# A conditioned linear layer and a mixture of experts: gathered rows kept in two column halves, left-half products first, and the matrix engine's expert stage ordered by hand

## The chip, the cores and the metric

The kernel runs on one core of a Trainium2 chip. The time is that of the device, in microseconds (us), for one execution; lower is better. Several executions are timed, and one more is recorded by the hardware profiler, from which all rows below come. The engines are PE (TensorE, the matrix engine; its weight loads are shown as PEld), DVE (VectorE), ACT (ScalarE), POOL (GpSimd) and SP (SyncE, which here only issues DMAs). Each engine takes its instructions in the order in which they stand in its program, and an instruction waits for the semaphores that it names.

## The reference

There are four sequences of 1024 tokens with 512 columns. Each sequence is multiplied by a weight matrix picked by its category, and a bias is added. The result goes through a mixture of 8 experts with 512 slots each: a router picks one expert per token, tokens get a rank among those with the same expert, those of rank 512 and more are dropped, and each expert does two layers (512 to 2048, ReLU, 2048 to 512). The output is weighted by the probability of the choice and added to the input.

```python
xl = einsum('bsd,bdh->bsh', x, W[cat]) + b[cat][:, None, :]
xf = xl.reshape(4096, 512)
probs = softmax(xf @ Wr); eidx = argmax(probs); p_tok = probs[eidx]
rank = (number of earlier tokens with the same expert)
keep = rank < 512                       # 512 slots for each of 8 experts
xe = xf[dispatch]                       # [8, 512, 512], rows by expert and slot
h  = maximum(einsum('ecd,edf->ecf', xe, W1), 0)
ye = einsum('ecf,efd->ecd', h, W2) * p_tok[dispatch] * valid
out = x + scatter(ye)
```

All is float32.

## The kernel before, in words

**Seven products.** Every matrix product is done by a scheme with seven block products in place of eight (Strassen's, in Winograd's form): both operands are cut into two by two blocks, sums and differences of the blocks are made first (`sums`, `differences`, `sum_w`, `sum_w1`, `sum_w2`, on DVE), and the products k = 1 to 7 are added up in three PSUM banks called x, y and z (`BANK`). Products 1, 6, 7 and 4 go, in this order, into bank x. Between them the bank is copied out (by DVE in `linear`, by ACT in `first_layer`), so product 6 can be added only when the copy after product 1 is done, 7 after the copy of 6, and 4 after that of 7. Product 2 has bank z; 5 and 3 share bank y.

**Linear stage** (lines 178 to 537). PE and SP follow an order written by hand: `ORDER` lists, for one sequence b, pairs (g, k) of a half g of its tokens and a product k, and `beside` says what PE does after each of the fourteen (transposes of x and of the weights, the router, `choose` and `rank`). A block of the result that is finished is written by SP into `xc_dram` in HBM (`done`), a row of which has 512 columns. `choose` (DVE) picks the expert of each of 1024 tokens, and builds up counts `past`, one step of 128 x 8 numbers after the other; `rank` needs two PE products with these counts, and then POOL scatters (token, probability) pairs into `slots` in HBM, eight indirect DMAs for each sequence. After the last sequence `keep_warm` lets PE do seven products on zeros.

**Between the stages** (lines 539 to 546). ACT's queue loads `slots` into `table`, POOL makes row numbers of it, and `gather` (POOL, indirect DMAs) fetches the 512 rows of expert 0 from `xc_dram`, 128 at a time into a tile of 128 x 512. `transpose_rows` transposes them on PE, four 128 x 128 blocks for each tile, and DVE copies them out (L610) and makes the differences.

**Expert stage** (lines 704 to 747). Here only SP's order is by hand. The order of PE, DVE, ACT and POOL is made by the framework's scheduler, from dependencies and estimates, and need not be that of the text. For each expert, `first_layer(e, g, k)` runs over four groups g of hidden columns with seven products of eight passes each (four matmuls; a float32 matmul is recorded as two passes). `second_layer(e, k)` has seven products in two halves of sixteen passes each, one for `at` = 0 and one for `at` = 1, that lie in the same PSUM bank:

```python
for at in range(HC):                  # L671, HC = 2
    for m in range(NG * HB):
        nc.tensor.matmul(ps[:, at, :], ...)
    if k in (1, 2):
        add(ps, 0, at, 0)             # DVE, L667: rows += ps * probability
```

After each half, `add` (DVE, L667) reads the bank and adds it to the rows; for k = 7 two such additions follow (bank x and bank y), for k = 5 none. The framework makes a write into a bank wait for the reads of it that stand before it in the text, though they are of the other half. Among the second-layer products stand the last two first-layer products of the expert (k = 4 and 3 of group 3) and `transpose_rows` of the next expert, and the scheduler laid such work between the two halves of a product. `fetch` gathers, early in each expert, its input rows and the next expert's rows (eight indirect DMAs on POOL).

The functions that the change touches, with their line numbers:

Of the kernel before, what the change touches and what calls it, by code (L numbers as in the profile page):

```python
# [22 lines left out]
def kernel(  # L23
# [97 lines left out]
    xc_dram = dram.tile([T, D], F32, name="xc_dram")  # L121

    table = const.tile([P, E, SC, ROW], F32, name="table")
# [54 lines left out]
    with (  # L178
# [7 lines left out]
        tc.tile_pool(name="xco", bufs=1) as xco,  # L186
# [184 lines left out]
        def rank(b):  # L371
# [12 lines left out]
            nc.vector.scalar_tensor_tensor(at, best, -float(CAP), r, ALU.mult, ALU.add)  # L384
            dest = rt.tile([P, GT], I32, tag="dest", bufs=B, name=f"dest_{b}")
            nc.vector.scalar_tensor_tensor(dest, at, float(E * CAP), over, ALU.add, ALU.add)
# [13 lines left out]
        def linear(b, g, k):  # L400
# [3 lines left out]
            ps = bank(ps_x, key, k, [P, 2, HD], "xc", bufs=2 if BANK[k] == "x" else 1)  # L404
# [20 lines left out]
            def block(i, j):  # L425
                return xco.tile([P, 2, HD], F32, tag=f"c{i}{j}", name=f"xc{i}{j}_{c}")

            def done(t, i, j):
                at = c * CT + i * HT
                nc.sync.dma_start(  # L430
                    out=xc_dram[at : at + HT, j * HD : (j + 1) * HD].rearrange(
                        "(j p) d -> p j d", p=P
                    ),
                    in_=t,
                )

            if k in (1, 6, 7):
                banks[key, k] = parts.tile([P, 2, HD], F32, tag=f"s{k}", name=f"s{k}_{b}_{g}")
                plus_bias(banks[key, k], 0 if k == 1 else 1)
            if k in (2, 3):  # L440
                t = block(0, int(k == 3))
                latest[0] = nc.vector.tensor_tensor(
                    t, ps, banks.pop((key, 1 if k == 2 else 6)), ALU.add
                )
                done(t, 0, int(k == 3))
            if k == 7:
                t = block(1, 1)
                nc.vector.tensor_tensor(t, banks[key, "y"], banks.pop((key, 7)), ALU.add)
                done(t, 1, 1)
            if k == 4:  # L450
                t = block(1, 0)
                plus_bias(t, 0)
                done(t, 1, 0)
# [5 lines left out]
        )  # L459

# [38 lines left out]
            (2, 7): [(X, 3, 6)],  # L499
            (2, 8): [(X, 3, 7), (RS, 3, 0)],  # L500
            (2, 9): [(behind, sum_w, 3)],
            (2, 10): [(R, 3, 1)],
            (2, 12): [(RS, 3, 1), (choose, 3)],
            (2, 11): [(behind, sum_w1, 0, 0)],
            (3, 2): [(rank, 3)],
            (3, 4): [(behind, sum_w1, 0, 1)],
            (3, 7): [(behind, sum_w1, 0, 2)],
# [12 lines left out]
        with tc.manual_schedule(engines={mybir.EngineType.PE, mybir.EngineType.SP}):  # L520
# [11 lines left out]
            for b in range(B):  # L532
                for i, (g, k) in enumerate(ORDER):
# [3 lines left out]
            keep_warm(ps_t, 7)  # L537

        nc.scalar.dma_start(
            out=table.rearrange("p e c r -> p e (c r)"),  # L540
            in_=slots.rearrange("(e p c) r -> p e (c r)", e=E, c=SC),
        )

        token = table.rearrange("p e c r -> p (e c) r")[:, :, 1]
        nc.gpsimd.tensor_scalar(src_row, token, FAR, float(T - 1), ALU.add, ALU.min)
        nc.gpsimd.tensor_scalar(dst_row, token, FAR, None, ALU.add)
# [32 lines left out]
    def gather(e, pool, source, into, at):  # L579
        for c in range(SC):  # L580
            n = e * SC + c
            into[n] = pool.tile([P, D], F32, tag="rows", name=f"rows_{n}")
            nc.gpsimd.indirect_dma_start(  # L583
                out=into[n],
                out_offset=None,
                in_=source,
                in_offset=bass.IndirectOffsetOnAxis(ap=at[:, c : c + 1], axis=0),
            )

    def fetch(e):  # L590
# [4 lines left out]
        gather(e, xr, xf, residual, at[:, 0:SC])  # L595
# [3 lines left out]
    def transpose_rows(e, c):  # L599

        if c == 0:
            xes[e] = xep.tile([P, 7, HK, HC * P], F32, tag="xe", name=f"xe_{e}")
        t = xes[e]
        r = rows.pop(e * SC + c)
        ps = ps_e.tile([P, KC, P], F32, tag="t", name=f"ps_e_{e}_{c}")
        for kc in range(KC):
            nc.tensor.transpose(ps[:, kc, :], r[:, kc * P : (kc + 1) * P], ident)  # L607

        half, at = divmod(c, HC)
        nc.vector.tensor_copy(  # L610
            t[:, 2 * half : 2 * half + 2, :, at * P : (at + 1) * P].rearrange(
                "p b k n -> p (b k) n"
            ),
            ps,
        )
        if c == SC - 1:
            differences(nc.vector, *(t[:, k, :, :] for k in (0, 2, 1, 3, 4, 5, 6)))
# [6 lines left out]
    def first_layer(e, g, k):  # L624
# [16 lines left out]
        if k in (1, 6, 7):  # L641
            banks[key, k] = snap.tile([P, HB, HC * P], F32, tag=f"s{k}", name=f"s{k}_{e}_{g}")
# [16 lines left out]
    def second_layer(e, k):  # L659
# [4 lines left out]
        def add(ps, half, at, part):  # L664
# [3 lines left out]
                row, ps[:, at, :], table[:, e, half * HC + at, 0:1], row, ALU.mult, ALU.add  # L668
# [35 lines left out]
    with tc.manual_schedule(engines={mybir.EngineType.SP}):  # L704
        gather(0, xg, xc_dram, rows, src_row)
        for c in range(SC):
            transpose_rows(0, c)
        for e in range(E):
            for g in range(NG):
                first_layer(e, g, 1)  # L710
                first_layer(e, g, 2)
                if g > 0:
                    first_layer(e, g - 1, 4)
                    first_layer(e, g - 1, 3)
                    ahead = e * NG + g - 1 + W1G
                    if ahead < E * NG:
# [62 lines left out]
```

## Time and profile before

| | |
|---|---|
| median of 3 runs | 971.0 us (967.38 to 971.63) |
| the profiled execution | 969.31 us, its span 967.5 us |
| mean granted PE clock in it | 0.995 of full speed |
| PE busy | 950.1 us, 98% of the span |
| DVE, ACT, POOL busy | 472.7, 171.0, 139.1 us |
| HBM | read 105.96 MB, written 25.23 MB |
| linear stage | from the start to about 153 us |
| one expert | 99.0 us (expert 1 begins at 272.01, expert 2 at 371.04) |
| last PE instruction | ends at 962.3 us |

A page of the profile gives the busy time of each engine, the groups of instructions, and what ended the idle time before an instruction. In the rows of the order of time, the first number is the start in us, the second how long it took, then engine, line of the program, operation, the tiles (written<-read) with buffer numbers left out, and in brackets idle time of the engine just before it with what ended it. Ends of matmuls are modelled and overlap the next start by some 0.15 us, so the pace of PE is read from starts.

### The profile page before, as it was taken

What the parts mean: (1) busy time and instruction counts of PE and PEld (TensorE: products, weight loads), DVE (VectorE), ACT (ScalarE), POOL (GpSimd) and SP (SyncE); (2) the same over time, 40 slices, a digit from 0 to 9 for tenths busy, and PEclk for the clock granted to TensorE, in tenths of its full rate; (3) what the DMA queues carried; (4) which work ended last, traced back from release to release, by engine and by line L of the source; (5) the groups of instructions that cost most, each with busy time, mean ns of one, the idle gap of its engine ahead of it and who ended that gap; (6) DMA issues with size and microseconds to landing.
All of it is one profiled execution on the core that took longest, in us unless ns stands there. A gap on an engine that the chain in (4) does not pass through costs nothing.

```text
span 967.5 us, 11249 instructions
## 1 busy us (share of the span) xinstructions
PE 950.1 (98%) x4570; PEld 812.2 (84%) x4570; DVE 472.7 (49%) x822; ACT 171.0 (18%) x289; POOL 139.1 (14%) x141
## 2 busy tenths in 40 slices
PE   9999988999999999999999999999999999999997
PEld 5788776888888888888888888888888888888886
DVE  4656574374337522762276317731673157325621
ACT  3233200320023002310231013101320132003200
POOL 0043332200022001200130013001300130012001
PEclk9999998999999999999999999999999999999999
DMA  9389223399134313532253225313532352332001
GB/s 323 115 166 227 90 81 93 132 400 337 60 131 159 131 55 114 173 107 74 84 175 127 82 93 174 130 48 128 174 101 73 127 174 71 104 126 87 1 0 44
DMA packets 95509, 123.18 MB, mean 127 GB/s; under 512 B 8820, under 2 KB 82548, under 8 KB 95266
## 3 DMA queue, kind: packets, MB, share of 16 engines
q1 hardware_dynamic: 85042, 97.54, 31.6%
q0 software_dynamic: 8704, 24.85, 7.8%
q8 instruction: 36, 0.59, 0.2%
q10 hardware_dynamic: 1712, 0.08, 0.1%
q14 instruction: 15, 0.12, 0.1%
HBM read 105.96 MB, written 25.23 MB: 136 GB/s over the span
## 4 chain that ended last, share of the span: by engine, by line
PE 58%; issue 17%; DVE 4%; DMA 2%; POOL 1%; SPq 1%; POOLq 0%; ACT 0%; DVEq 0%
PE hx L630 17%; PE yx L673 16%; PE yy L673 9%; PE hy L630 8%; PE hz L630 4%; PE yz L673 3%; DMA w_b<-in_L_ffn_W_dram 2%; PE ps_e L607 1%; POOL out_dram L694 1%; POOL rows L583 1%; SPq L566 1%; DMA rows<-xc_dram,src_row 0%; DVE h L150 0%; DVE h L151 0%; DVE h L149 0%
## 5 line engine op out<-in xcount | busy, mean ns | idle before, releaser
L630 PE MATMUL hx<-xe,w 128*128 128x256 f32 x1024 | 242.8, 382 | 1.4 <-ACT s L643 1.4
L630 PEld LDWEIGHTS hx<-xe,w 128*128 128x128 f32 x1024 | 195.3, 192 | 27.6 <-ACT s L643 1.8
L643 ACT COPY s<-hx 128x512 f32<-128x512 f32 x96 | 55.9, 582 | 437.7 <-PE hx L630 437.7
L630 PE MATMUL hy<-xe,w 128*128 128x256 f32 x512 | 122.1, 380 | 0.0
L673 PE MATMUL yx<-w_t,h 128*128 128x256 f32 x512 | 119.9, 380 | 1.2 <-DVE rows L667 1.2
L673 PE MATMUL yx<-w_b,h 128*128 128x256 f32 x512 | 116.6, 381 | 1.1 <-DVE rows L667 1.1
L694 POOL DMA_INDIRECT out_dram<-rows,dst_row x32 | 31.9, 998 | 572.1 <-DVE rows L667 572.1
L673 PEld LDWEIGHTS yx<-w_b,h 128*128 128x128 f32 x512 | 95.8, 190 | 16.5 <-DVE rows L667 3.7
L673 PEld LDWEIGHTS yx<-w_t,h 128*128 128x128 f32 x512 | 95.4, 190 | 15.9 <-DVE rows L667 2.0
L630 PEld LDWEIGHTS hy<-xe,w 128*128 128x128 f32 x512 | 97.4, 190 | 13.3 <-DVE h L646 0.4
L667 DVE SCALAR_TENSOR_TENSOR rows<-yx,table,rows 128x256 f32<-128x256 f32 x64 | 31.0, 484 | 140.2 <-PE yx L673 140.2
L647 ACT ACTIVATE h<-h 128x512 f32<-128x512 f32 x96 | 60.5, 630 | 203.0 <-DVE h L646 203.0
L646 DVE TENSOR_TENSOR h<-hy,s 128x512 f32<-128x512 f32 x64 | 44.2, 691 | 98.8 <-PE hy L630 54.8
L630 PE MATMUL hz<-xe,w 128*128 128x256 f32 x256 | 61.7, 380 | 0.0
L673 PE MATMUL yz<-w_b,h 128*128 128x256 f32 x256 | 58.7, 383 | 0.4
L673 PE MATMUL yy<-w_b,h 128*128 128x256 f32 x256 | 58.4, 381 | 0.0
L673 PE MATMUL yy<-w_t,h 128*128 128x256 f32 x256 | 57.9, 380 | 0.0
L583 POOL DMA_INDIRECT rows<-in_x_dram,at x32 | 40.2, 1257 | 122.7 <-DVE at L594 93.0
L673 PEld LDWEIGHTS yz<-w_b,h 128*128 128x128 f32 x256 | 48.1, 190 | 9.5 <-DVE rows L667 3.4
L630 PEld LDWEIGHTS hz<-xe,w 128*128 128x128 f32 x256 | 48.9, 191 | 6.6
L673 PEld LDWEIGHTS yy<-w_b,h 128*128 128x128 f32 x256 | 47.6, 190 | 8.1 <-DVE rows L667 1.4
L673 PEld LDWEIGHTS yy<-w_t,h 128*128 128x128 f32 x256 | 48.2, 190 | 6.2
(118 smaller groups left out, 894.7 us busy)
## 6 DMA issues: line engine op xcount, KB each, us to landing
w<-in_L_ffn_W_dram SPq DMA_DIRECT2D x64, 512.0 KB, 4.3
w_b<-in_L_ffn_W_dram SPq DMA_DIRECT2D x32, 1024.0 KB, 5.5
x<-in_x_dram SPq DMA_DIRECT2D x8, 1024.0 KB, 9.7
xc_dram<-xc SPq DMA_DIRECT2D x32, 256.0 KB, 4.1
out_dram<-in_x_dram SPq DMA_DIRECT2D x2, 2816.0 KB, 22.4
cw<-in_L_cond_W_dram SPq DMA_DIRECT2D x4, 1024.0 KB, 11.2
out_dram<-in_x_dram SPq DMA_DIRECT2D x1, 2560.0 KB, 16.0
cb<-in_L_cond_b_dram SPq DMA_DIRECT2D x4, 256.0 KB, 9.9
```

Source lines behind the costliest of these rows:

```text
L566: nc.sync.dma_start(out=t[k], in_=w2[e, i * F // 2 : (i + 1) * F // 2, j * D // 2 : (j + 1) * D // 2].rearrange("(m p) d -> p m d", p=P),)
L583: nc.gpsimd.indirect_dma_start(out=into[n], out_offset=None, in_=source, in_offset=bass.IndirectOffsetOnAxis(ap=at[:, c : c + 1], axis=0),)
L607: nc.tensor.transpose(ps[:, kc, :], r[:, kc * P : (kc + 1) * P], ident)
L630: nc.tensor.matmul(ps[:, j, :], lhsT=w1s[e, g][:, LEFT[k], kc, j * P : (j + 1) * P], rhs=xes[e][:, RIGHT1[k], kc, :], start=(k in OPENS an ...
L643: nc.scalar.copy(banks[key, k], ps)
L646: latest[0] = nc.vector.tensor_tensor(into, ps, part, ALU.add)
L647: nc.scalar.activation(into, into, AF.Relu)
L667: nc.vector.scalar_tensor_tensor(row, ps[:, at, :], table[:, e, half * HC + at, 0:1], row, ALU.mult, ALU.add)
L673: nc.tensor.matmul(ps[:, at, :], lhsT=hs[e, m // HB][:, LEFT[k], m % HB, at * P : (at + 1) * P], rhs=w2s[e][RIGHT2[k]][:, m, :], start=(k ...
L694: nc.gpsimd.indirect_dma_start(out=of, out_offset=bass.IndirectOffsetOnAxis(ap=dst_row[:, n : n + 1], axis=0), in_=residual.pop(n), in_off ...
```

## The change

- `xc_dram` is two tensors of 256 columns instead of one of 512. `gather` fetches rows in as many parts as it is given sources: all left halves, then all right halves, so the next expert's rows take eight indirect DMAs instead of four. The input rows are still fetched whole.
- `slots` and `table` are laid out with the expert innermost, and the index arithmetic in `rank` follows. Each partition loads one run of `slots` instead of eight.
- In `linear`, the finished blocks are added up in place in the tiles of the bank copies, which get two buffers; the pool `xco` goes. The last sequence has its own order (`ORDERS`): for each half of the tokens products 1, 2, 6, 7, 4, then 5, 5, 3, 3; with it, `choose` and `rank` of the last sequence move ahead in `beside`. The last product 5 has a bank in another pool. Two idle products follow the stage, not seven.
- `transpose_rows` can do the left or the right half of the columns alone. For expert 0 a loop does so three times, each followed or interrupted by products of groups 0 and 1: left halves with k = 1, left halves with k = 5, right halves with k = 2; products 4 and 3 and 6 and 7 of these groups follow from the main loop, whose middle part is now the function `between`.
- The bank copy after product 1 of the first layer has two buffers.
- In the expert stage PE's order, too, is that of the text.

```diff
-    xc_dram = dram.tile([T, D], F32, name="xc_dram")
-    table = const.tile([P, E, SC, ROW], F32, name="table")
+    xc_dram = [dram.tile([T, HD], F32, name=f"xc{j}_dram") for j in range(2)]
+    table = const.tile([P, SC, E, ROW], F32, name="table")
...
-            nc.vector.scalar_tensor_tensor(at, best, -float(CAP), r, ALU.mult, ALU.add)
+            nc.vector.scalar_tensor_tensor(at, r, float(E), best, ALU.mult, ALU.subtract)
...
-            ps = bank(ps_x, key, k, [P, 2, HD], "xc", bufs=2 if BANK[k] == "x" else 1)
+            if (b, g, k) == (B - 1, 1, 5):
+                banks[key, "y"] = ps_l.tile([P, 2, HD], F32, tag="m", name="xcy_last")
+                ps = banks[key, "y"]
+            else:
+                ps = bank(ps_x, key, k, [P, 2, HD], "xc", bufs=2 if BANK[k] == "x" else 1)
...
             if k in (2, 3):
-                t = block(0, int(k == 3))
-                latest[0] = nc.vector.tensor_tensor(
-                    t, ps, banks.pop((key, 1 if k == 2 else 6)), ALU.add
-                )
+                t = banks.pop((key, 1 if k == 2 else 6))
+                latest[0] = nc.vector.tensor_tensor(t, ps, t, ALU.add)
                 done(t, 0, int(k == 3))
-            if k == 7:
-                t = block(1, 1)
-                nc.vector.tensor_tensor(t, banks[key, "y"], banks.pop((key, 7)), ALU.add)
+            if k == (7 if b < B - 1 else 5):
+                t = banks.pop((key, 7))
+                nc.vector.tensor_tensor(t, banks[key, "y"], t, ALU.add)
...
+        ORDERS = [ORDER] * (B - 1) + [
+            [(g, k) for g in range(2) for k in (1, 2, 6, 7, 4)]
+            + [(g, k) for k in (5, 3) for g in range(2)]
+        ]
...
-            (2, 7): [(X, 3, 6)],
-            (2, 8): [(X, 3, 7), (RS, 3, 0)],
+            (2, 7): [(X, 3, 6), (X, 3, 7)],
+            (2, 8): [(R, 3, 1), (RS, 3, 0)],
             (2, 9): [(behind, sum_w, 3)],
-            (2, 10): [(R, 3, 1)],
-            (2, 12): [(RS, 3, 1), (choose, 3)],
+            (2, 10): [(RS, 3, 1), (choose, 3)],
             (2, 11): [(behind, sum_w1, 0, 0)],
-            (3, 2): [(rank, 3)],
-            (3, 4): [(behind, sum_w1, 0, 1)],
-            (3, 7): [(behind, sum_w1, 0, 2)],
+            (3, 0): [(rank, 3)],
+            (3, 5): [(behind, sum_w1, 0, 1)],
+            (3, 9): [(behind, sum_w1, 0, 2)],
...
-            keep_warm(ps_t, 7)
+            keep_warm(ps_t, 2)
...
-            out=table.rearrange("p e c r -> p e (c r)"),
-            in_=slots.rearrange("(e p c) r -> p e (c r)", e=E, c=SC),
+            out=table.rearrange("p c e r -> p (c e r)"),
+            in_=slots.rearrange("(p s) r -> p (s r)", p=P),
...
+    def gather(e, pool, sources, into, at):
+        n = D // len(sources)
+        for j, source in enumerate(sources):
+            for c in range(SC):
...
+                nc.gpsimd.indirect_dma_start(
+                    out=into[e * SC + c][:, j * n : (j + 1) * n],
...
+    def transpose_rows(e, c, parts=range(2)):
...
+        for kc in range(n * HK):
+            nc.tensor.transpose(ps[:, kc, :], r[:, (lo + kc) * P : (lo + kc + 1) * P], ident)
...
         if c == SC - 1:
-            differences(nc.vector, *(t[:, k, :, :] for k in (0, 2, 1, 3, 4, 5, 6)))
+            b11, b21, b12, b22, t1, t2, t4 = (t[:, k, :, :] for k in range(7))
+            if 0 in parts:
+                nc.vector.tensor_tensor(t1, b12, b11, ALU.subtract)
+            if 1 in parts:
+                nc.vector.tensor_tensor(t2, b22, t1, ALU.subtract)
+                nc.vector.tensor_tensor(b12, b22, b12, ALU.subtract)
+                nc.vector.tensor_tensor(t4, b21, t2, ALU.subtract)
...
-    with tc.manual_schedule(engines={mybir.EngineType.SP}):
+    with tc.manual_schedule(engines={mybir.EngineType.PE, mybir.EngineType.SP}):
         gather(0, xg, xc_dram, rows, src_row)
-        for c in range(SC):
-            transpose_rows(0, c)
+        for k, part in ((1, [0]), (5, [0]), (2, [1])):
+            for c in range(SC):
+                transpose_rows(0, c, part)
+                if (k, c) in ((1, HC - 1), (5, SC - 1), (2, HC - 1)):
+                    for g in range(2):
+                        first_layer(0, g, k)
         for e in range(E):
             for g in range(NG):
+                if e == 0 and g < 2:
+                    between(e, g)
+                    first_layer(e, g, 6)
+                    first_layer(e, g, 7)
+                    continue
                 first_layer(e, g, 1)
                 first_layer(e, g, 2)
...
+                between(e, g)
                 first_layer(e, g, 6)
```

## The prediction

> **What bounds the kernel now.** I read the engine table first, then the waits of the matrix engine (PE), then the order of time at the two places that the change rewrites. Page, head and engine table:
>
> ```profile
> span 967.5 us, 11249 instructions
> ...
> PE 950.1 (98%) x4570; PEld 812.2 (84%) x4570; DVE 472.7 (49%) x822; ACT 171.0 (18%) x289; POOL 139.1 (14%) x141
> ```
>
> PE is busy for 950.1 of 967.5 us, so time can be gained only in the remaining 17, or where PE is busy at a low clock or with idle products; whatever lets PE wait is added whole. PE in the view of waits (who waited for whom: us, times, longest):
>
> ```profile
> PE ps_e L607 <- DMA rows<-xc_dram,src_row: 2.5, 3, 1.4
> PE yx L673 <- DVE rows L667: 2.2, 4, 0.6
> ```
>
> The first row is the gather ahead of expert 0, the second the second layer waiting for VectorE (DVE) to read a bank. The order of time around the gather (start us, us, engine, line):
>
> ```profile
> 153.27 6.17 PE L69 MATMUL ps_idle<-idle 128*128 128x512 f32 x14
> 157.34 1.06 POOL L583 DMA_INDIRECT rows<-xc_dram,src_row  x1 [1.49 <-DMA xc_dram<-xc]
> 160.80 0.66 PE L607 MATMUL ps_e<-ident,rows 128*128 128x128 f32 x4 [1.36 <-DMA rows<-xc_dram,src_row]
> ...
> 168.90 1.94 PE L630 MATMUL hz<-xe,w 128*128 128x256 f32 x8
> ```
>
> and the clock there (stretch, us, busy us of PE, PEld, DVE, ACT, POOL, granted clock, DMA):
>
> ```profile
> 161.00:162.00 1.00, 0.46 (x4) 0.22 (x3) 0.50 (x1) 0.00 (x0) 0.79 (x1) 1.00 0.66 213
> 162.00:163.00 1.00, 0.70 (x4) 0.70 (x4) 0.19 (x1) 0.00 (x0) 0.16 (x1) 0.58 0.66 201
> ...
> 168.00:169.00 1.00, 1.00 (x4) 0.78 (x3) 0.97 (x3) 0.00 (x0) 0.00 (x0) 0.50 0.00 0
> 169.00:170.00 1.00, 1.00 (x6) 0.90 (x5) 0.96 (x2) 0.58 (x1) 0.00 (x0) 1.00 0.00 0
> ```
>
> A product of eight passes takes 1.726 us at full clock (303.09 to 311.72 holds five), four transposes 0.434. From the last linear product (153.27) to `hz` at 168.90 PE needs 1.74 + 1.73, so some 12 us are lost: gather, copies, half clock for 6.8 us. That is what can be won here.
>
> The other place is the second layer. Expert 2, first two products (k=1 and k=2, two halves each):
>
> ```profile
> 412.48 3.62 PE L673 MATMUL yx<-w_b,h 128*128 128x256 f32 x16
> 415.93 1.89 PE L630 MATMUL hx<-xe,w 128*128 128x256 f32 x8
> 417.65 1.03 PE L630 MATMUL hy<-xe,w 128*128 128x256 f32 x4
> 418.05 0.48 DVE L667 SCALAR_TENSOR_TENSOR rows<-yx,table,rows 128x256 f32<-128x256 f32 x1
> 418.59 3.72 PE L673 MATMUL yx<-w_b,h 128*128 128x256 f32 x16
> ...
> 423.01 3.62 PE L673 MATMUL yz<-w_b,h 128*128 128x256 f32 x16
> ...
> 428.76 0.48 DVE L667 SCALAR_TENSOR_TENSOR rows<-yz,table,rows 128x256 f32<-128x256 f32 x1
> 429.29 3.72 PE L673 MATMUL yz<-w_b,h 128*128 128x256 f32 x16
> ```
>
> The second half of a product never starts before L667 has read the first half (same bank): 418.53 to 418.59, 429.24 to 429.29. In between PE does first-layer products, transposes and the next product, put there by the scheduler. The last expert, with less to put there, shows the bare wait:
>
> ```profile
> 938.85 3.62 PE L673 MATMUL yx<-w_b,h 128*128 128x256 f32 x16
> 942.51 0.48 DVE L667 SCALAR_TENSOR_TENSOR rows<-yx,table,rows 128x256 f32<-128x256 f32 x1 [9.01 <-PE yx L673]
> ...
> 943.04 3.72 PE L673 MATMUL yx<-w_b,h 128*128 128x256 f32 x16 [0.58 <-DVE rows L667]
> ```
>
> The slot of sixteen passes ends at 938.85 + 3.45 = 942.30, the next starts at 943.04: 0.74 us.
>
> **The change, part by part.** The largest part is one word: PE joins the engines with an order by hand in the expert stage. In the built program the sixteen passes of each product then stand together, with no filler between halves.
>
> *Second layer.* Work and DVE's order up to each L667 are as before, so I take each wait from where L667 stands behind its producer. Of experts 1 to 6: k=1, half one ends at 415.93, half two starts at 418.59: 2.66 (DVE still has w2 sums and an h total ahead). k=2: L667 follows L630 k=3 by nine DVE operations (h total, four w1 sums, four h sums); from the end of k=3 (423.01) to half two (429.29) are 6.28, less half one, 3.45: 2.83. k=6, k=7, k=3 and k=4: 0.74 each, 2.96. k=5 has no reader. Half one of k=3 needs the second L667 of k=7, behind one L667 and one copy of transposed rows: 0.2 start + 0.53 + 0.60 + 0.48 + 0.05 = 1.86, less the four transposes, 0.43: 1.43. Sum 9.88 an expert, 59.3 for six. Expert 0: k=1 1.52 (217.48 to 219.00), k=2 229.94 - 225.15 - 3.45 = 1.34, the rest 4.39: 7.2. Expert 7 (no transposes, no w1 sums): 0.74 + 1.33 + 2.96 + 1.26 = 6.3. All 72.8. Before, this stretch runs from 214.03 to 962.0, 748.0 us; its products and transposes are 386.7 + 338.5 + 3.5 + 12.2 = 740.8; 7.2 of waits were there. **Net +65.6.** Bounds: with all waits bare 5.7 an expert, 46.6 in all, +39.4; above, the sum itself plus the clock.
>
> *Clock.* Idle of 1.36 and 0.84 us in the stretch before 162.2 let it fall to 0.50 for 6.8 us; two waits of 1.5 at 128.7 and 132.4 did not. Twelve waits of 2.66 or 2.83 are new. Bounds: none falls, 0; each falls for 6.8, 12 x 3.4 = +41. After 162.2 PE stayed partly idle for two more us; behind these waits it is full at once, so I take half the duration (3.4 us low, 1.7 lost). Whether a wait of 2.7 suffices lies between the 1.5 that did not and the 2.2 in two pieces that did, and may hang on where it falls in time, so I take half of the twelve: 6 x 1.7 = **+10**, an estimate.
>
> [...]
>
> *Last linear batch.* `choose` comes after (2,10) instead of (2,12), `rank` after (3,0): PE asks for `past` at 126.8, DVE has it at about 129.7 (its order still holds ten 0.6 us operations between the seven `past`), wait 2.9, as before (1.53 + 1.45). But k=6, 7, 4 now follow each other in one bank, each behind a 0.69 copy (L418): 0.2 + 0.69 + 0.05, 0.95 to 1.05 four times, 3.95. The stage ends at about 156.6 instead of 153.27. Bounds: two of the copies free, +1.4; DVE's w1 sums ahead of all, +6.
>
> *Scatter, table, gather.* The scatters start at about 131.8 (135.63 before): eight, 1.28 apart, last ends 142.0; the table load was issued 4.9 after that, src_row came 4.4 later: 151.3. The load in one 256 B run per partition instead of eight of 32 B may save up to 2 (shortest landing of an `xc_dram` write 2.1 against 4.3). Left halves of the rows are written by 153.75 (copy ends 150.6, landing 3.1 as at 154.2 to 157.34). Left gathers are issued 153.75 to 157.6, landing 157.2 to 161.1 (3.46 each); right ones, behind the write of k=3, from 160.65, landing 164.1 to 168.0.
>
> *Expert 0, from 156.6 to the first product of group 2* (189.67 - 1.73 = 187.95 before, 34.7 after the linear stage). Two idle products 1.73 (five dropped), twelve products 20.7, twelve pairs of transposes 2.6: the loop transposes the left half twice, as part [0] stands for k=1 and again for k=5. Waits: left copy 0.7; the second pass of left copies, two banks deep, 163.45 to 167.15 less its transposes 2.8; right copies 0.65; t2 behind two h totals and two copies 1.95; three bank snapshots with nothing between (k=6, 7, 4 of group 0, 6, 7 of group 1; copy 0.58) at 0.83, 2.5. Sum 33.7, so group 2 starts at 190.3, 2.3 late. A fall of the clock in the 2.8 us stretch is as likely as not: **+3**. Bounds: every wait hidden, 25.0 instead of 34.7, -9.7 + 3.3 = -6.4; clock low for 6.8 and right gather 3 late, +9.
>
> *At nothing:* index arithmetic (same two operations), in-place sums and second buffers (a buffer comes back after some 24 us, its write lands in 4.1), four more gathers per expert on POOL (4 x 1.27; POOL is 14% busy, the queue behind them is the output scatter, some 40 us later, and the transposes wait for rows landed 25 us earlier; if that cover went, 5 us an expert). SP's order keeps its transfers; w1 and w2 loads follow PE.
>
> Sum against the execution's own 969.31 (span 967.5 + 1.8, 1.7 below the median of 971.0 and inside 967.38 to 971.63): 969.3 + 65.6 + 10 + 3 = **1048 us**.
>
> **Rivals.** (a) Other side: PE's new order costs nothing per expert, since DVE is free in time, and the hidden gather decides: 969.3 - 6.4 = 963. It needs under 0.8 us an expert; one bare wait is 0.74, and there are six, so the three bare waits of the last expert speak against it. For it: DVE is 49% busy. (b) All waits bare, DVE having caught up: 969.3 + 39.4 + 3 = 1012. Against: DVE runs without a gap from 398 to 418. For: a slower PE leaves it time. (c) The clock falls at each long wait: 969.3 + 65.6 + 3 + 41 = 1079. For it: 2.2 us of idle sufficed at 162.2.
>
> **How the numbers follow.** Forecast 0.70 (1025 to 1066), (a) 0.03, (b) 0.12, (c) 0.12, anything else 0.03. The range 1018 to 1068 leaves out (a), (c) and half of (b), 2 in 10. About 0.5% is what a measurement can tell from no change: faster 0.03, same 0.01, slower 0.96.
>
> **What would show it.** Waits of yx, yy and yz for L667's counterpart: some 50, 60 to 75 us, against 2.2. In an expert, 2.7 and 2.8 us idle in k=1 and k=2, 0.74 in the others; from expert to expert 108 us (99.0 before: 272.01 to 371.04). Stretches of clock 0.50, about six. Linear stage ending near 156.6, left gather issued near 154, group 2 near 190. I am wrong if waits between halves are absent (then a), or 0.74 at k=1 and k=2 (b), or if an expert takes 108 but the clock never falls (969.3 + 65.6 + 3 = 1038).

## The result, and the profile after

The changed kernel takes 1055.65 us in the median of five executions (1055.23 to 1059.47), the kernel before, run beside it, 971.0 (967.38 to 971.87): 1.0886 times as long, 95% interval 1.086 to 1.0911. The forecast was 1048, with a range of 1018 to 1068. The profiled execution took 1055.48 us, 86.2 more than that of before (969.31).

The page of the changed kernel, span and engine table:

```profile
span 1053.7 us, 11265 instructions
...
PE 964.3 (92%) x4568; PEld 812.4 (77%) x4568; DVE 475.4 (45%) x831; ACT 171.2 (16%) x289; POOL 174.6 (17%) x173
```

PE is busy for 14 us more with the same products (eight more transposes, five fewer idle products), and the span has grown by 86: what is new is that PE stands still. The view of waits of PE says for whom (line 694 is the second layer's product, 688 the DVE instruction that reads its bank; us, times, longest):

```profile
PE yx L694 <- DVE rows L688: 30.8, 32, 2.5
PE yz L694 <- DVE rows L688: 18.3, 8, 2.7
PE yy L694 <- DVE rows L688: 13.9, 16, 1.2
PE hx L649 <- ACT s L664: 3.7, 4, 1.7
PE xcx_lin L413 <- DVE s L423: 3.5, 4, 1.0
PE rk L375 <- DVE past L356: 2.5, 1, 2.5
PE hx L649 <- DVE xe L634: 1.9, 1, 1.9
```

The first three rows are 56 waits and 63.0 us, against four waits and 2.2 us before. The idle time in such a row is counted from the modelled end of the product before, some 0.16 us late; from starts, the 56 waits are 72.1 us. Expert 2 in order of time, the lines that answer to the block of expert 2 in the prediction:

```profile
437.97 3.62 PE L694 MATMUL yx<-w_b,h 128*128 128x256 f32 x16
443.55 0.48 DVE L688 SCALAR_TENSOR_TENSOR rows<-yx,table,rows 128x256 f32<-128x256 f32 x1
444.08 3.72 PE L694 MATMUL yx<-w_b,h 128*128 128x256 f32 x16 [2.50 <-DVE rows L688]
...
451.10 3.62 PE L694 MATMUL yz<-w_b,h 128*128 128x256 f32 x16
456.84 0.48 DVE L688 SCALAR_TENSOR_TENSOR rows<-yz,table,rows 128x256 f32<-128x256 f32 x1
457.38 6.76 PE L694 MATMUL yz<-w_b,h 128*128 128x256 f32 x16 [2.66 <-DVE rows L688]
```

The second half of product 1 starts at 444.08, 0.05 us after the DVE instruction ended, as before; but nothing lies between the halves, so 444.08 - (437.97 + 3.45) = 2.66 us are lost, and 457.38 - (451.10 + 3.45) = 2.83 in product 2. Two smaller things stand in the same rows. A product behind a wait takes 3.72 where the others take 3.62: its second pass comes 0.1 us late, 56 times. And the last row takes 6.76: the clock fell during that wait. The same place by stretches (us, busy us of PE, PEld, DVE, ACT, POOL, granted clock, DMA):

```profile
453.32:456.74 3.42, 1.39 (x7) 0.89 (x5) 3.42 (x6) 0.00 (x0) 0.00 (x0) 1.00 1.01 303
456.74:460.15 3.41, 2.77 (x7) 2.24 (x8) 0.58 (x2) 0.00 (x0) 0.00 (x0) 0.50 0.72 243
460.15:463.56 3.41, 3.41 (x10) 2.69 (x9) 0.00 (x0) 0.00 (x0) 0.00 (x0) 0.50 0.01 5
463.56:466.98 3.42, 3.42 (x19) 3.04 (x18) 1.13 (x2) 0.00 (x0) 0.00 (x0) 1.00 0.50 125
```

From 456.74 to 463.56 the clock is at half, two stretches of 3.41 us, and full again after that. The opening of expert 0 in order of time, from the linear stage's end to product 7 of group 0:

```profile
157.46 1.88 PE L69 MATMUL ps_idle<-idle 128*128 128x512 f32 x4
159.18 0.60 PE L622 MATMUL ps_e<-ident,rows 128*128 128x128 f32 x4
160.41 3.72 PE L649 MATMUL hx<-xe,w 128*128 128x256 f32 x16 [0.63 <-DVE xe L623]
...
166.45 0.77 PE L622 MATMUL ps_e<-ident,rows 128*128 128x128 f32 x4 [0.82 <-DVE xe L623]
168.47 3.72 PE L649 MATMUL hy<-xe,w 128*128 128x256 f32 x16 [1.25 <-DVE xe L632]
...
179.31 2.82 PE L649 MATMUL hx<-xe,w 128*128 128x256 f32 x8 [1.89 <-DVE xe L634]
182.80 3.78 PE L649 MATMUL hx<-xe,w 128*128 128x256 f32 x8 [0.68 <-ACT s L664]
```

The gather no longer holds PE up: no wait here names a DMA. PE waits for DVE's copies and differences and for ACT's snapshots instead, and the clock falls there too (3.78 us for eight passes, 1.89 at full clock). Product 1 of group 2 starts at 195.27, against 187.95 before.

The whole 86.2 us, in three stretches read from PE's starts (before, after): up to expert 0's second layer 214.03, 222.67, **+8.6**; from there to PE's last pass 748.0, 823.4, **+75.4**; behind that 5.5, 7.65, **+2.1**. The middle one is 72.1 of waits, 5.6 of late second passes (56 x 0.1) and 4.7 of low clock, less the 7.2 that this stretch had lost before: 75.2.

### The profile page after: what moved, and what is told of

It is laid out like the page before. It is cut to its first block, busy times and chain, and to the rows that moved or that the text cites. A ratio compares the mean times of both kernels' runs of the same rounds, so it can differ in the third digit from the quotient of the medians.

```text
span 1053.7 us, 11265 instructions
## 1 busy us (share of the span) xinstructions
PE 964.3 (92%) x4568; PEld 812.4 (77%) x4568; DVE 475.4 (45%) x831; ACT 171.2 (16%) x289; POOL 174.6 (17%) x173
## 3 DMA queue, kind: packets, MB, share of 16 engines
q1 hardware_dynamic: 85042, 97.54, 27.9%
## 4 chain that ended last, share of the span: by engine, by line
PE 65%; issue 18%; DVE 13%; DMA 2%; POOL 2%; ACT 0%; POOLq 0%; SPq 0%; DVEq 0%
PE yx L694 15%; PE hx L649 14%; PE yy L694 8%; PE hy L649 7%; PE xcx_lin L413 5%; PE hz L649 4%; PE yz L694 2%; PE xcy_lin L413 2%; DVE rows L688 2%; DMA w_b<-in_L_ffn_W_dram 2%; PE ps_xT L244 1%; PE xcz_lin L413 1%; PE ps_idle L69 1%; POOL rows L594 1%; PE ps_e L622 1%
## 5 line engine op out<-in xcount | busy, mean ns | idle before, releaser
L694 PE MATMUL yx<-w_b,h 128*128 128x256 f32 x512 | 118.9, 386 | 21.6 <-DVE rows L688 21.6
L694 PE MATMUL yx<-w_t,h 128*128 128x256 f32 x512 | 117.4, 382 | 9.2 <-DVE rows L688 9.2
L694 PE MATMUL yz<-w_b,h 128*128 128x256 f32 x256 | 61.7, 397 | 18.3 <-DVE rows L688 18.3
L594 POOL DMA_INDIRECT rows<-xc_dram,at x56 | 57.9, 1035 | 17.1 <-issue 14.6
```

The costliest lines, as they stand in the source:

```text
L594: nc.gpsimd.indirect_dma_start(out=into[e * SC + c][:, j * n : (j + 1) * n], out_offset=None, in_=source, in_offset=bass.IndirectOffsetOnA ...
L694: nc.tensor.matmul(ps[:, at, :], lhsT=hs[e, m // HB][:, LEFT[k], m % HB, at * P : (at + 1) * P], rhs=w2s[e][RIGHT2[k]][:, m, :], start=(k ...
```

## The experiments

The theory: PE's order in the text costs the time, since a half of a second-layer product may not write a bank before DVE has read the other half, and the scheduler's filler between the halves is gone. The rivals: the half gathers, the banks and the boundary cost it; or DVE is behind in general, so that waits would only move. The runs were made on several chips; the kernel before, run beside each, took from 970.2 to 975.5 us there, so ratios to it are given, with 95% intervals. In five of them (halves interleaved, idle products, sum moved, left half once, two banks) ACT's snapshot stands still for 3.0 to 4.5 us at about 210 us, for something that the profile does not show, and PE waits 2.0 to 3.4 us behind it. Neither kernel of the change has this, so in these five runs a few us of time say little, and the views of waits say more.

**Everything of the change but the order of the experts.** PE's order is by hand only up to expert 0's second group.

```diff
+        for g in range(2):
+            between(0, g)
+            first_layer(0, g, 6)
+            first_layer(0, g, 7)
+
+    with tc.manual_schedule(engines={mybir.EngineType.SP}):
         for e in range(E):
```

> TensorE's order is the text only up to expert 0's second column group; every other product is placed by the scheduler, as before. Theory (the text's order in the second layers is what costs): the 72 us of waits of after's second-layer products and the 5.6 us of slow second passes behind them go, the 7 us that before has come back, so 1055.5 - 72.1 - 5.6 + 7.2 - 4 (clock) = about 981 us, 975 to 987. What is left over before is the boundary, some 8 to 10 us. Rival (the half gathers, the new bank places or the tables cost it): the order is not the cause and the time stays above 1040 us. A result in between, 1000 to 1030, would say that the waits are partly made by something else than the order.

981.48 us, 1.0083 of before (1.0059 to 1.0108). The view of waits of PE has the second layer back where it was:

```profile
PE yx L694 <- DVE rows L688: 2.2, 4, 0.6
```

So it is the order of the experts that costs the time, and the rest of the change costs 8 us.

**The order alone, in the kernel before.**

```diff
-    with tc.manual_schedule(engines={mybir.EngineType.SP}):
+    with tc.manual_schedule(engines={mybir.EngineType.PE, mybir.EngineType.SP}):
```

> The kernel before with one edit, TensorE kept in the order of the text in the expert stage, and no half gathers, no new bank places, no new tables. Theory: the second layers get after's waits, 72.1 + 5.6 - 7.2 = +70.5 us, and the clock falls in a few of them for 3 to 5 us: 971 + 70.5 + 4 = about 1045 us, 1035 to 1055; the first groups of expert 0 may add some us, because the products 1 and 2 wait for all four rows there. Rival (the order needs the other edits to cost anything): below 1000 us.

1051.4 us, 1.0793 (1.0774 to 1.0812). Its view of waits has the three rows of the changed kernel nearly to the digit (line 673 is the product here, 667 the reader):

```profile
PE yx L673 <- DVE rows L667: 30.7, 32, 2.5
PE yz L673 <- DVE rows L667: 18.3, 8, 2.7
PE yy L673 <- DVE rows L667: 13.9, 16, 1.2
```

The two parts add up: 1.0083 x 1.0793 = 1.0883, and the whole change measured 1.0886.

**The text's order kept, but other work written between the halves.**

```diff
-            second_layer(e, 1)
+            second_layer(e, 1, [0])
             first_layer(e, NG - 1, 4)
             first_layer(e, NG - 1, 3)
...
-            for c, k in enumerate((2, 6, 5, 7)):
-                second_layer(e, k)
-                if e + 1 < E:
-                    transpose_rows(e + 1, c)
+            second_layer(e, 1, [1])
+            second_layer(e, 2, [0])
+            second_layer(e, 6, [0])
+            second_layer(e, 2, [1])
+            second_layer(e, 6, [1])
...
```

> After, still in the text's order everywhere, but the second layer's products are written by halves with other work between the two halves of one bank: product 1 left, group 3's products 4 and 3, product 1 right, 2 left, 6 left, 2 right, 6 right, 5, 7 left, two transposes, 7 right, two transposes, 3 left, 4 left, 3 right, 4 right. Nothing is left out. Theory (a half waits for VectorE to have emptied the other half of its bank, and 1.7 us of other work hides that): nearly all of the 72 + 5.6 us goes, so 1055.5 - 75 = about 980 us, 975 to 990. Rival (the wait is for something else than the other half, such as VectorE being behind in general): the waits only move to other products and at least half of them stay, above 1015 us.

987.61 us, 1.0128 (1.0093 to 1.0163): of the 63.0 us in the rows of the second layer 6.9 are left. (PE also stands still for 5.4 us in three places with no cause in the profile, the one at 210 us among them.) Expert 1 there, in order of time:

```profile
335.79 3.62 PE L696 MATMUL yx<-w_b,h 128*128 128x256 f32 x16
339.25 3.62 PE L696 MATMUL yz<-w_b,h 128*128 128x256 f32 x16
342.70 3.62 PE L696 MATMUL yx<-w_t,h 128*128 128x256 f32 x16
346.15 3.62 PE L696 MATMUL yz<-w_b,h 128*128 128x256 f32 x16
349.61 3.62 PE L696 MATMUL yx<-w_t,h 128*128 128x256 f32 x16
```

The two halves of product 2 (`yz`) have half of product 6 between them, and no start is late. An order by hand is not slow in itself; this one had no filler.

**Product 2 in two banks, the order unchanged.** This takes away what makes PE wait, and nothing else.

```diff
         for at in range(HC):
+            if k == 2 and at == 1:
+                ps = ps_p.tile([P, HC, HD], F32, tag="z", bufs=2, name=f"yz2_{e}")
...
-                    start=(k in OPENS and at == 0 and m == 0),
+                    start=(k in OPENS and (at == 0 or k == 2) and m == 0),
...
```

> After, with the right half of product 2 of each second layer in a bank of its own (the other of the two that product 2 and the first layer's product 2 take in turn); the order of all engines stays, nothing is left out. Theory (TensorE may not write a bank that VectorE is still reading, and that alone makes the wait): the wait in the middle of product 2, 18.3 us over eight experts, goes whole with its slow second passes (0.8 us) and the fall of the clock behind one of them (3 us): -19 to -22 us against after, and no wait appears in front of product 6 over 0.3 us. Rival (TensorE waits because VectorE is late in general): the wait moves to product 6, and the time falls by under 8 us.

1039.96 us, 1.0682 (1.0643 to 1.072), so 0.0204 less than the changed kernel, 19.8 us. The row of `yz` is gone from the waits, those of `yx` and `yy` are as they were, and in order of time the two halves are one run of 32 passes:

```profile
442.23 3.72 PE L696 MATMUL yx<-w_b,h 128*128 128x256 f32 x16 [2.50 <-DVE rows L688]
...
449.24 7.07 PE L696 MATMUL yz<-w_b,h 128*128 128x256 f32 x32
```

Hence in product 2 DVE's delay alone holds nobody up; it is the shared bank that turns it into a wait.

**Why 2.8 us and not 0.74: DVE's queue.**

```diff
-            if e + 1 < E:
-                behind(sum_w1, e + 1, W1G - 2)
             for c, k in enumerate((2, 6, 5, 7)):
                 second_layer(e, k)
+                if k == 2 and e + 1 < E:
+                    behind(sum_w1, e + 1, W1G - 2)
```

> After, with the four sums of the next expert's first-layer weights (1.4 us of VectorE) taken out of their place ahead of product 2's halves and put behind product 2; nothing is left out. Theory (the wait in the middle of product 2 is 2.8 us and not 0.74 because VectorE first finishes the sums it stands behind): that wait falls to between 0.74 and 1.4 us in experts 1 to 6, so -8 to -12 us against after, and the waits in product 1 stay at 2.7 us. Rival (the long wait is a property of the bank or of the product): no change in the wait.

The row of `yz` falls from 18.3 to 11.1 us, that of `yx` stays at 30 (30.8, now 30.0):

```profile
PE yz L694 <- DVE rows L688: 11.1, 8, 1.5
```

The step is right, and its size, 7.2 us, a little under the 8 to 12 expected. The time, 1057.22 us, 1.0826 (1.0794 to 1.0858), is 6 us below the change's by the middle of two wide intervals, and does not settle it alone. In this profile the clock fell in the wait of product 1 in all six experts 1 to 6, for some 9.8 us against 4.7, and PE stood still 3.4 us at 210.80.

**Idle products in the twelve long waits.**

```diff
-            second_layer(e, 1)
+            second_layer(e, 1, [0])
+            if 0 < e < E - 1:
+                keep_warm(ps_e, 2)
+            second_layer(e, 1, [1])
...
-                second_layer(e, k)
+                second_layer(e, k, [0])
+                if 0 < e < E - 1 and k == 2:
+                    keep_warm(ps_e, 2)
+                second_layer(e, k, [1])
```

> After, with two idle products (1.73 us of TensorE's time) put between the two halves of products 1 and 2 of the second layers of experts 1 to 6; nothing is left out. Theory (TensorE stands still there for 2.7 us anyway, waiting for the other half of the bank): the time does not grow, although 12 x 1.73 = 20.8 us of work are added; the clock, which fell in two of these waits for some 4.7 us, stays up, so 0 to -5 us against after. Rival (the waits are made longer by whatever TensorE does, VectorE's work follows it): up to +21 us.

1058.97 us, 1.0844 (1.0805 to 1.0883): 20.8 us of work more, and no longer than the change (1.086 to 1.0911). The rows give it closely: `yx` and `yz` fall from 49.1 to 27.9 us, by 21.2.

```profile
PE yx L696 <- DVE rows L690: 19.9, 32, 0.8
PE yz L696 <- DVE rows L690: 8.0, 8, 1.2
```

None of the twelve waits has a fall of the clock in this profile. The one fall from the second layer of expert 0 on, at 649.38, follows another wait, of 2.26 us before a first-layer product.

**The left half of expert 0's rows transposed once.**

```diff
             for c in range(SC):
-                transpose_rows(0, c, part)
+                if (k, c) not in ((1, 2), (1, 3), (5, 0), (5, 1)):
+                    transpose_rows(0, c, part)
```

> After, with the left half of expert 0's rows transposed once instead of twice (products 1 and 5 use the same transposes), so 8 transposes and 5 VectorE instructions less in the opening; nothing else changes. Theory: the opening of expert 0 is a chain of transpose, copy and product without slack, so it is 2.5 to 3.5 us shorter, and the second layers stay as they are: 1052 to 1053 us by after's 1055.5. Rival (the right half's rows set the opening): no change, TensorE waits for the right half's rows instead.

By the time this is undecided: 1.0854 (1.0797 to 1.0911), and in the profile, 1060.71 us, the clock fell in five of the long waits and cost 8.2 us. By the order of time the opening, from the linear stage's end to product 1 of group 2, is 35.4 us (161.01 to 196.36) against 37.8, so 2.5 of the expected 2.5 to 3.5 us are there.

**The half gathers alone, in the kernel before.**

```diff
-    xc_dram = dram.tile([T, D], F32, name="xc_dram")
+    xc_dram = [dram.tile([T, HD], F32, name=f"xc{j}_dram") for j in range(2)]
...
-    def gather(e, pool, source, into, at):
+    def gather(e, pool, sources, into, at):
+        n = D // len(sources)
+        for j, source in enumerate(sources):
...
```

> The kernel before with one edit: the rows for the experts are kept and gathered by halves of their columns, as in after (eight indirect DMAs instead of four for each expert, left halves first); every order stays, and rows are still transposed whole. Theory: the last instructions of every kernel with half gathers so far stand 6.6 us before the end instead of 4.4, with one transfer of instructions in between, so the tail is 2.1 us longer here too; the last row tile of expert 0 lands after eight issues 1.27 us apart instead of four, so TensorE starts expert 0 up to 5 us later; in the other experts nothing changes. Together +4 to +7 us, 1.004 to 1.007 of before. Rival (the half gathers cost nothing, and the boundary's 8 us come from the two orders alone): 0.998 to 1.002, and no longer tail.

974.68 us, 1.0044 (1.003 to 1.0058). The rows of expert 0 are waited for longer (4.8 us in the view of waits, 2.5 before), and from the linear stage's end to product 2 of group 0 it takes 1.9 us more (153.67 to 171.20; 153.27 to 168.90 before). The other 2.1 us are behind PE's last pass. The last scatter in order of time, and what the DMA engines moved from 966 to 973:

```profile
966.35 0.98 POOL L697 DMA_INDIRECT out_dram<-rows,dst_row  x1 [3.32 <-DVE rows L670]
```

```profile
DMA  0000000000299930000000000000000000000001
GB/s 0 0 0 0 0 0 0 0 0 0 94 445 374 445 141 0 0 0 0 0 0 0 0 0 0 0 0 0 0 0 0 0 0 0 0 0 0 0 0 47
...
q14 instruction: 1, 0.01, 0.3%
```

The rows have landed by 968.7, and at 972.9 one transfer of instructions is the last thing that happens. The kernel before has none there and ends 4.4 us after its last scatter begins, instead of 6.6. All eleven kernels profiled here that have half gathers end with such a transfer, 6.6 us after (to 0.1), and the order alone ends without it, 4.5 us after. Why the transfer is needed is not shown.

**Both orders mended.** The second layers go back to the scheduler. In the last linear batch the two halves of the tokens alternate, so that a snapshot has a product to hide behind, and `rank` comes two products later; expert 0 transposes its left half once, and its first two groups alternate.

```diff
-            [(g, k) for g in range(2) for k in (1, 2, 6, 7, 4)]
-            + [(g, k) for k in (5, 3) for g in range(2)]
+            [(0, 1), (0, 2), (1, 1), (0, 6), (1, 2), (1, 6)]
+            + [(g, k) for k in (7, 4, 5, 3) for g in range(2)]
...
-            (3, 0): [(rank, 3)],
+            (3, 2): [(rank, 3)],
...
-                [P, HB, HC * P], F32, tag=f"s{k}", bufs=1 + (k == 1), name=f"s{k}_{e}_{g}"
+                [P, HB, HC * P], F32, tag=f"s{k}", bufs=2, name=f"s{k}_{e}_{g}"
...
+        rows_and([(0, 0), (1, 0)], (0, 1))
+        rows_and([(2, 0), (3, 0)], (1, 1), (0, 5))
+        rows_and([(0, 1), (1, 1)], (1, 5))
+        rows_and([(2, 1), (3, 1)], (0, 2), (1, 2), (0, 6), (1, 6), (0, 7), (1, 7))
+        between(0, 0)
+        between(0, 1)
...
```

(`rows_and(parts, *products)` calls `transpose_rows(0, c, [half])` for each pair in `parts`, then `first_layer(0, g, k)` for each product.)

> The second layers placed by the scheduler (as in the run that kept only the opening by hand) and the two orders by hand mended: the last linear batch alternates its two row groups (products 1, 2 | 1 | 6 | 2 | 6 | 7, 7 | 4, 4 | 5, 5 | 3, 3), the rank products come two products later, the left half of expert 0's rows is transposed once, and its first two groups alternate in products 1, 5, 2, 6, 7, with the transposes between them. Theory (the boundary costs 8 us over before because TensorE waits there for snapshots, ranks and copies, and half gathers by themselves bring rows earlier): the linear stage ends about 6.4 us earlier than in after (2.5 for the rank, 3.5 for the snapshots, 0.4 of slow second passes), the opening of expert 0 has next to no waits, and the third group starts some 8 us before the kernel before does: 0.992 of before, 0.986 to 0.997. Rival (the half gathers land so late that TensorE waits for the right half's rows, or the scheduler's experts give the gain back): 0.999 to 1.006.

969.21 us, 0.993 of before (0.9907 to 0.9953). The linear stage now ends at 151.02, and the opening has 2.3 us of waits in all. But there is a new one behind it, and the clock falls there for some 3 us more; in order of time:

```profile
199.28 1.23 DVE L157 TENSOR_TENSOR w_t<-w_b,w_b 128x1024 f32<-128x1024 f32 x1 [7.49 <-DMA w_b<-in_L_ffn_W_dram]
200.42 0.68 DVE L667 TENSOR_TENSOR h<-hz,s 128x512 f32<-128x512 f32 x1
...
206.28 3.78 PE L649 MATMUL hx<-xe,w 128*128 128x256 f32 x8 [5.54 <-ACT s L664]
```

PE is early, so a sum of second-layer weights stands at the head of DVE's queue and waits 7.49 us for its load; the total of group 3 that stands behind it, though ready, comes late, ACT's snapshot after that, and PE waits 5.54. The same chain, smaller, is in the changed kernel (DVE waits 3.76 us for that load, PE 1.03 and 1.67). Two ways out, each tried alone on top of this version:

```diff
-            if g == 1:
-                load_w2(0)
...
         gather(0, xg, xc_dram, rows, src_row)
...
+        load_w2(0)
```

> The version with both orders mended, with expert 0's second-layer weights loaded right after the gather is asked for (about 155 us) instead of behind the fourth group's first-layer weights (180 us). There the sums of these weights stood at the head of VectorE's queue waiting 7.5 us for the load, a total of group 3 behind them, a snapshot behind that, and TensorE waited 5.5 us, with the clock falling behind it for about 3 us. Theory: these 8.5 us go: 969.2 - 8.5 = about 961 us, 0.985 of before, 0.981 to 0.990. Rival (the 4 MB of weights share the DMA engines with the right half's rows and delay them): the gain is lost in the opening, 0.990 to 0.997.

```diff
-        if g >= 2:
-            behind(sum_w2, e, g - 2)
+        if g >= 2 and (e > 0 or g == 3):
+            behind(sum_w2, e, g - 2 if e > 0 else 0)
...
+            if e == 0:
+                behind(sum_w2, 0, 1)
             second_layer(e, 1)
```

> The version with both orders mended, with the load where it was, but expert 0's two rounds of second-layer weight sums placed one group later in VectorE's order. Theory: the total of group 3 no longer stands behind sums that wait for a load, so the 5.5 us wait and the 3 us of fallen clock go as well, 0.983 to 0.989 of before. Rival (the sums then come late for the second layer's product 6, or crowd the rows of products 1 and 2): 0.989 to 0.997.

964.48 us, 0.9891 (0.9872 to 0.991), and 964.89, 0.9893 (0.9871 to 0.9916): both beat before by 1.1%; the second lies on the border between the ranges of its theory and its rival. The wait is gone in both: from product 1 of group 2 to the second layer it takes 12.1 and 13.0 us, and 19.6 in the version with both orders mended. That the gain is 4 us and not 8.5 is ahead of it, where group 2 starts 5.9 and 3.1 us later than in that version: in these two profiles the linear stage ends 1.3 and 1.5 us later, the clock falls behind the wait for the first rows, and, with the early load, those rows come later. With the early load, in order of time:

```profile
158.34 0.69 PE L622 MATMUL ps_e<-ident,rows 128*128 128x128 f32 x2 [3.10 <-DMA rows<-xc_dram,src_row]
159.54 3.78 PE L649 MATMUL hx<-xe,w 128*128 128x256 f32 x8 [0.52 <-DVE xe L623]
```

## Why the prediction was right, point by point

- **The mechanism and the waits of the second layer.** Forecast 72.8 us in all, measured 72.1; by place, in experts 1 to 6, 2.66 and 2.66 (product 1), 2.83 and 2.83 (product 2), 0.74 and 0.74 (products 6, 7, 3, 4), 1.43 and 1.34 (start of product 3). The way to these numbers holds: take from the profile of before where the reader stands behind its producer in DVE's queue, and take away the filler. Two runs show the cause from both sides (the order alone 1.0793, all but the order 1.0083), and the two-bank run shows the mechanism.
- **The late second pass** of 0.1 us behind each wait was not in the sum: 5.6 us. The row to read it from was there, 3.72 against 3.62 at 943.04 of before; the prediction shows it and has no term for it.
- **The clock** was put at +10, six falls of 1.7. It was 4.7: two falls, one of 3.1 and one of 1.6. The price of one stretch of 3.4 us at half clock was right (1.7, measured 1.6), but one of the falls lasted two stretches. The count was not right, and could not be had from the profile of before: the five kernels here that have these long waits of product 1 or 2 show two falls (the changed kernel), three (the order alone), six (the sum moved), five (the left half once) and two (two banks) in them. That the clock falls behind idle times of under 3 us is what the row at 162.2 of before had shown, with 1.36 and 0.84 us; here it fell behind waits of 2.83 and 2.66.
- **The boundary** was put at +3 (upper bound +9) for the start of group 2, and was +7.3. In the linear stage the four snapshot waits, read from starts, cost 4.2 and the late second passes behind them 0.4, together 4.6 for the 3.95 worked out, and the stage ends 4.2 later instead of 3.3. The 3.3 was too low by the prediction's own terms: 3.95, less 0.1 at the rank, is nearer 3.9. `src_row` is made at 145.19, six earlier than worked out, because the table load was issued 1.1 us after the scatters instead of 4.9 and used 1.8 later instead of 4.4. That gains nothing: the left gather also needs the last left block, whose write lands at 153.44, and starts at 154.55. Then the step "expert 0, from 156.6 to the first product of group 2", 33.7 us, took 37.8: the fall of the clock that was called as likely as not came (2.7 us), and the waits are 1.4 longer: 0.6 of it late second passes, 0.4 in the second pass of left copies, the rest some 0.1 in each of the others.
- **Groups 2 and 3** lose another 1.3 us in the changed kernel, by the queue of DVE standing at a load. This was in no step.
- **"At nothing"** held for the experts and failed at the end: the half gathers bring 2.1 us behind PE's last pass, as the run with them alone shows.

Summed: waits -0.7, second passes +5.6, clock -5.3, up to the second layer +5.6, tail +2.1, together +7.3, and the miss was 7.5. That the forecast came so near is in part luck: errors of 5 us of both signs met. The range would have held without it (1048 and the errors of one sign alone, 13.3, are 1061); the mechanism alone gave 1035 (969.3 + 65.6).

Rival (a), that the order costs nothing, fell by the 63.0 us of waits; what it named, the gather that comes to be hidden, is real, but the gain of 6 us came only with both orders mended, and no run separates the gather's share in it. Rival (b), bare waits, fell by the 2.66 and 2.83; two of its readings were loose, and neither decides: DVE does pause between 398 and 418, for 0.84 us at 407.50, and eight experts at 5.7 are 45.6, not 46.6. Rival (c), a fall in every long wait, fell by the two falls in twelve.

## What to carry to other kernels

Before fixing an engine's order by hand, look for places where that engine writes a buffer that another engine is still reading: the scheduler may have been hiding the wait there (2.2 us of waits before, 63.0 after), and the text has to bring its own filler (6.9 us left with the halves interleaved), or the second half its own bank (19.8 us less). The price is read beforehand from the position of the reader in its queue, not from how busy its engine is (72.8 us forecast in this way, 72.1 measured). And an engine that comes early finds new heads of queues: a sum that waits for a load holds up whatever ready work stands behind it (here 7.49 us on DVE and then 5.54 on PE).

## What the runs showed of the hardware

- **The clock fell for 3.41 or 6.83 us at a time.** In the changed kernel's record of the granted clock it is at half from 180.26 for 6.83 us, from 456.74 for 6.83 and from 555.73 for 3.41, starts that are 276.48 and 98.99 us apart (81 and 29 times 3.413); in that of before from 162.16 for 6.83; and in both once more behind PE's last pass, to the end of the record. In the 3.41 us ahead of the three falls PE was busy for 1.52, 1.39 and 1.29 us, and ahead of the one in before for 1.35. From 893.64 to 897.05 of the changed kernel it was busy for 1.47, and no fall followed: the wait there, in product 2 of expert 6, is 2.83 us, as long as the one before the fall at 456.74. So the length of a wait alone does not tell whether the clock falls behind it; what does is not shown. From 456.74 to 460.15 PE was busy for 2.77 us, and the clock was at half for the next 3.41 too; from 555.73 to 559.14 it was busy for 3.04, and the clock was full after that.
- **The count of falls differs between kernels with the same waits of product 1.** In the run with the sums moved, the second layers of experts 1 to 7 start 109.49, 109.37, 109.30, 109.26, 109.25 and 109.24 us apart, and the clock fell in the wait of product 1 of all six experts 1 to 6, at 339.27, 448.50, 557.73 and on, 109.23 apart (32 times 3.413). In the changed kernel an expert without a fall takes 108.97 us (108 were forecast), and two waits of twelve had one. That it is the place of a wait in time that decides is the author's reading of these distances; no run moves a wait by itself.
- **An indirect gather in more pieces changed the end of the program**, by one transfer of 0.01 MB of instructions, with 2.1 us (6.6 for 4.4 us from the last scatter on). Which engine's instructions they are, the trace does not say.
- **The table load in one run of 256 bytes for each partition** was issued 1.1 us after the last scatter in the changed kernel, and the row numbers were made of it 1.8 us later (1.7 to 2.1 in all kernels with this load); with eight runs of 32 bytes it was 4.9 and 4.4 in the kernel before (3.0 to 4.4 in the three kernels with it). No run changes the load alone, so that the shape of the load makes the difference is likely, not shown.
